# Sums of squares of a gated group norm: a row of ones as weights and a way through DRAM, in a one-core Mamba-2 kernel

## The chip, the cores and the metric

The kernel runs on one core of a Trainium2 chip, in fp32. The metric is the device time of one execution in microseconds (us): before the change 1738.12 us, the median of three runs (1737.26 to 1739.64). Smaller is better.

The core has five engines with an instruction list each: PE (TensorE, the matmuls; PEld are its weight loads), DVE (VectorE), ACT (ScalarE), POOL (GpSimd) and SP (SyncE, which only issues transfers). Each works its own list strictly in order; they wait for each other by semaphores. A transfer is issued from an engine's list, and whoever reads its data waits for its landing.

## The reference, cut to what matters

```python
y = (Y_diag + Y_off).reshape(b, l + pad, NH, HD) + D_res     # a Mamba-2 layer, 4 batches x 256 tokens
y = y[:, :l].reshape(b, l, DIN)                              # DIN = 8192
y = y * jax.nn.silu(gate)
yg = y.reshape(b, l, G, GROUP_SIZE)                          # G = 8 groups of 1024
var = jnp.mean(yg * yg, axis=-1, keepdims=True)
y = (yg * jax.lax.rsqrt(var + EPS)).reshape(b, l, DIN) * norm_w
return y @ out_proj_w.T
```

In front of it stands a layer norm and beside it an FFN with ternary weights, whose silu is multiplied to the result; they are not touched. The change concerns `var`: for each of 1024 tokens and each of 8 groups the sum of 1024 squares.

## The kernel before, in words

The 8192 channels are 64 tiles of 128 channels (partitions) by 1024 tokens; eight tiles are a group. After a front part (layer norm, FFN, B and C, early decay rows), a loop over the 64 tiles runs three stages shifted against each other. The program's order in each engine's list is written out by hand, so the order of the code is the order of the lists.

In step i:
- tile i is projected (`product`, L170, matmul at L173) by Strassen-like products into px, pq and pz; its convolution and silu follow on VectorE and ACT (L181, L186). The last product of pq (L173, "pq<-xnT,s") accumulates onto the pq that the add at L898 has read before;
- tile i-1 gets its sequence mixing: `decay_scan` (L188, a scan on VectorE) over the decay rows m that `load_rows` (L612, transfer at L617) fetched one step earlier, an exponential (L630), products with the scores (`meet`, L632), transposes through the one PSUM bank of the pool `ps_t`, the v products on VectorE (L648, L657), and `y_products` (L671, matmul at L684). From step 10 on the scan of tile i's first m is made at the beginning of step i (L850), before tile i-1's `meet`, and that of its second m at the end (L953);
- tile i-2 is gated (`y_gate`, L687), stored to DRAM (L825), squared on ACT (`square`, L862). The first square of a group is the tile sqacc; later ones are added to it by an accumulating transfer from POOL (L938);
- the finished group is projected by the output weights (`out_first`, L743, matmul at L740): factor sums of the loaded group on VectorE (`left_sums`, L808 and L720 to L723), then four products in an even and three in an odd step; ACT moves them out (L794), scaled by rs, into sa, sb and sc, and POOL adds them to DRAM. sc has two buffers.

A group ends so: steps 9, 17, 25, ... square its last tile. In the following step (10, 18, 26, ...) `norm_sums` (L699) makes eight matmuls with sqacc as weights and a column of ones as the moving side, so that the sums stand on the tokens' partitions, [128 x 8]; ACT takes the square root (L705), VectorE the reciprocal rs (L922), and ACT's leaves of that step use it. The eighth group is summed in the same way after the loop.

In SP's list, `load_rows` for step i+1 stands at the end of step i. Its first load needs a free buffer of five and goes out in the middle of step i; its second waits until `y_products` of step i has read tile i-1's m. Behind it stand the weights w and off-diagonal decay rows mo of the next step, and the store of the gated tile.

Of the kernel before, what the change touches and what calls it, by code (L numbers as in the profile page):

```python
# [43 lines left out]
F32 = mybir.dt.float32  # L44
# [3 lines left out]
ALU = mybir.AluOpType  # L48
PSUM = bass.MemoryType.PSUM

P = 128
NB = 4
L = 256
NC = 2
T = NB * L
NT = T // P
# [5 lines left out]
G = 8  # L62
# [3 lines left out]
CT = DIN // P  # L66
PER_G = CT // G
HG = PER_G // 2
HH = HID // 2
# [5 lines left out]
LEAD = 10  # L75
EARLY = 10
HALF = T // 2
ROW = T + NB * P


@with_exitstack
def mixer_ffn(ctx: ExitStack, tc: tile.TileContext, x, in_w, conv_w, conv_b, dt_bias, a_log, d_col,
              norm_w, out_w, gate_t, up_t, down_t, gate_s, up_s, down_s, out):
    nc = tc.nc

    const = ctx.enter_context(tc.tile_pool(name="const", bufs=1))
    small = ctx.enter_context(tc.tile_pool(name="small", bufs=3))
    dram = ctx.enter_context(tc.tile_pool(name="dram", bufs=1, space=bass.MemoryType.DRAM))
    ps_proj = ctx.enter_context(tc.tile_pool(name="ps_proj", bufs=3, space=PSUM))
    ps_t = ctx.enter_context(tc.tile_pool(name="ps_t", bufs=1, space=PSUM))  # L90
    ps_o = ctx.enter_context(tc.tile_pool(name="ps_o", bufs=2, space=PSUM))
# [2 lines left out]

    eps = const.tile([P, 1], F32, name="eps")
    nc.gpsimd.memset(eps, EPS)
    one = const.tile([P, 1], F32, name="one")
    nc.gpsimd.memset(one, 1.0)
    ident = const.tile([P, P], F32, name="ident")
    make_identity(nc, ident)  # L100
# [17 lines left out]
    dt_tail = mc.tile([P, NB, NH], F32, name="dt_tail")  # L118
    gm = mc.tile([P, ROW], F32, name="gm")
    xc = mc.tile([P, 4, KT // 2, HALF], F32, name="xc")  # L120
    xpad = mc.tile([P, NB, PADW], F32, name="xpad")
    nc.gpsimd.memset(xpad[:, :, 0:TAPS - 1], 0.0)
    rows = dram.tile([NH, ROW], F32, name="rows")
    ffn = dram.tile([T, HID], F32, name="ffn")
    acc = dram.tile([T, HID], F32, name="acc")
    gated = dram.tile([CT, P, T], F32, name="gated")
    early = dram.tile([2 * EARLY, P, T], F32, name="early")
    scores = dram.tile([G, P, ROW], F32, name="scores")

    def load_w(*tiles):  # L130
        w = wp.tile([P, 2, KT, P], F32, name="w")
        for n, i in enumerate(tiles):
            nc.sync.dma_start(w[:, n], in_w[i])
        return w
# [23 lines left out]

    x11, x12, x21, x22 = [xnT[:, k:k + 2, h:h + HALF] for k in (0, 2) for h in (0, HALF)]
    t1, t2, t3, t4 = [xc[:, n] for n in range(4)]  # L160

    def halves(xpad):
        return [xpad[:, 2 * h:2 * h + 2, TAPS - 1:] for h in range(2)]

    xpad_h = halves(xpad)

    def by_batch(v):
        return v.rearrange("p (b l) -> p b l", l=L)
# [23 lines left out]
    def front(pre, one_of, fp, f2, hp, ep):  # L192
# [11 lines left out]
        bT, cT = [one_of.tile([P, NB, L], F32, name=n) for n in ("bT", "cT")]  # L204
        sc = one_of.tile([P, ROW], F32, name="sc")
        wdt = one_of.tile([P, KT, P], F32, name="wdt")
# [69 lines left out]
        def split_x():  # L276
            return [hp.tile([P, KT, HALF], F32R, name=n) for n in ("xh", "xl")]

# [5 lines left out]
        def project_exact(w, xh, xl):  # L284
            pp = ps_proj.tile([P, HALF], F32, name="pp", tag="proj")
            for k in range(KT):
                for part in (xh, xl):
                    nc.tensor.matmul(pp, w[:, k * P:(k + 1) * P], part[:, k, :],  # L288
                                     start=(k == 0 and part is xh),
                                     stop=(k == KT - 1 and part is xl))  # L290
            return pp
# [26 lines left out]
        def dt_project(h):  # L318
            pd = ps_proj.tile([P, HALF], F32, name="pd", tag="proj")
            for k in range(KT):  # L320
                nc.tensor.matmul(pd, wdt[:, k, :], xnT[:, k, h * HALF:(h + 1) * HALF],  # L321
                                 start=(k == 0), stop=(k == KT - 1))
            nc.vector.tensor_scalar(z[:, h * HALF:(h + 1) * HALF], pd, bias, None, ALU.add)
# [285 lines left out]
    osp = main.enter_context(tc.tile_pool(name="osp", bufs=1, reuse_waits="tile"))  # L609
# [86 lines left out]

        return k // 2 if g in (0, G - 1) else max(k // 2, k - 2)

    def norm_sums(sqacc, pool=ps_o, tag="o"):  # L699
        pv = pool.tile([P, NT], F32, name="pv", tag=tag)  # L700
        for t in range(NT):
            nc.tensor.matmul(pv[:, t:t + 1], sqacc[:, t * P:(t + 1) * P], one,  # L702
                             start=True, stop=True)
        sd = small.tile([P, NT], F32, name="sd2")
        nc.scalar.activation(sd, pv, AF.Sqrt, bias=eps, scale=1.0 / (DIN // G))  # L705
        return sd


    def load_gated(g, b, tiles=PER_G):
        ya = yap.tile([P, PER_G, L], F32, name="ya")  # L710
        nc.sync.dma_start(ya[:, 0:tiles], gated[g * PER_G:g * PER_G + tiles, :,
                                                b * L:(b + 1) * L].rearrange("j p l -> p j l"))
        return ya
# [29 lines left out]
    def out_first(left, right, leave):  # L743

        a11, a12, a22, s1, s2, s4, s3 = left
        b11, b21, b22, tw1, tw2, tw3, tw4 = right
        px, pq = out_bank(), out_bank()
        out_product(px, a11, b11, True)
        yield leave(px, 0, 0, 0)
        out_product(pq, s1, tw1, True)  # L750
        yield leave(pq, 1, 1, 1)
        out_product(px, s2, tw2, False)
        yield leave(px, 0, 1, 0)
        out_product(pq, s4, b22, False)
        yield leave(pq, 0, 1, 1)

        out_product(px, s3, tw3, False)
        yield leave(px, 1, 1, 0)
        out_product(pq, a12, b21, True)
        yield leave(pq, 0, 0, 1)  # L760
        out_product(px, a22, tw4, False)
        yield leave(px, 1, 0, 0)
# [17 lines left out]
    with tc.manual_schedule():  # L780
        nc.sync.dma_start(gm, scores[0])
        ms, offs = {0: load_rows(0)}, {0: load_off(0)}
        xTs, gTs, yps, wos, rights, toms = {}, {}, {}, {}, {}, {}
        sqacc = sq = rs = ya = outs = left = nxt = ob = sa = sb = sc = None
        for i in range(CT):
            r, g = i % PER_G, i // PER_G
            here, old, older = True, i >= 1, i >= 2
# [20 lines left out]
            def left_sums():  # L808
                nonlocal ya, left
                ya = nxt  # L810
                left, sums = left_factors(ya)
                for make in sums:
                    make()

            if on % 2 == 0:
                ob = on // 2
# [6 lines left out]
            if older:  # L823
                yg = y_gate(yps.pop(i - 2), gTs.pop(i - 2))
                nc.sync.dma_start(gated[i - 2], yg.rearrange("p b l -> p (b l)"))  # L825
                if r == 1 and i >= PER_G and here:
                    nxt = load_gated((i - PER_G) // PER_G, 0)

            if here:
                a11, a12, a22, s1, s2, s4, s3 = a  # L830
                px, pq, pz = [p.tile([P, HALF], F32, name=f"p{n}", tag=tag) for n, p, tag in
                              (("x", ps_proj, "proj"), ("q", ps_proj, "proj"),
                               ("z", ps_proj if i else ps_t, "proj" if i else "t"))]
# [28 lines left out]
            def square():  # L862
                nonlocal sq, sqacc
                yf = yg.rearrange("p b l -> p (b l)")
                first = (i - 2) % PER_G == 0
                sq = sqp.tile([P, T], F32, name="sqacc" if first else "sq")
                nc.scalar.activation(sq, yf, AF.Square)  # L867
                if first:
                    sqacc = sq

            if older and fill:
                square()
# [6 lines left out]
            if old and fill:  # L879
                yps[i - 1] = y_begin(i - 1, xTs[i - 1])  # L880
            if og >= 0 and on == 0:
                sd = norm_sums(sqacc)
            for k in range(PER_G):
                if wg >= 0 and wn == come(wg, k) + 1:
                    wo = wos[wg][:, k, :]
# [3 lines left out]

            if og >= 0 and (here and on % 2 == 0 or i == CT - 1):
                left_sums()
            if wg >= 0 and wn == (PER_G - 1 if wg else PER_G - 3):
                rights[wg], toms[wg] = right_factors(wos[wg])
                toms[wg].pop(0)()
            if here:
                nc.vector.tensor_add(xpad_h[1], xpad_h[1], by_batch(pq))  # L898
            if old:
                vs = values_0(i - 1, tp0)  # L900
# [17 lines left out]
            if here:  # L918
                nc.vector.tensor_add(gT[:, HALF:], gT[:, HALF:], pq)
                if og >= 0 and on == 0:  # L920
                    rs = small.tile([P, NT], F32, name="rs2", bufs=2)
# [11 lines left out]
                    nc.scalar.activation(gT[:, HALF:], gT[:, HALF:], AF.Silu)  # L933
            if old:
                y_products(yps[i - 1], vs, ms.pop(i - 1), offs.pop(i - 1), fill)
            if older and (i - 2) % PER_G:
                if i - 2 < CT - 1:
                    nc.gpsimd.dma_start(sqacc, sq, accum_op=ALU.add)  # L938
                else:
                    nc.vector.tensor_add(sqacc, sqacc, sq)  # L940
            if here:
                conv_taps(i, xTs[i], xpad, (1, 2) if fill else (0, 1, 2))
                gTs[i] = gT
# [12 lines left out]
            if og >= 0 and on % 2:  # L956
# [3 lines left out]
                else:  # L960
                    nc.gpsimd.dma_start(rows_b, sa, accum_op=ALU.add)
                nc.gpsimd.dma_start(rows_b[:, 0, :], sb.rearrange("p n c -> p (n c)"),
                                    accum_op=ALU.add)
                nc.gpsimd.dma_start(rows_b[:, 1, HH:], sc, accum_op=ALU.add)
            elif og >= 0 and on < PER_G - 2:
                nxt = load_gated(og, ob + 1)
# [11 lines left out]
        last, ob = CT - 1, NB - 1  # L978
# [8 lines left out]
        sa = wp.tile([P, NC, KT, P], F32, name="w").rearrange("p n k m -> p n (k m)")  # L987
        sb = scp.tile([P, 3, KT // 2, P], F32, name="s")[:, 0:2].rearrange("p n k m -> p n (k m)")
        sc = osp.tile([P, HH], F32, name="sc", bufs=2)
        outs = out_first(left, rights[G - 2], leave)  # L990
# [3 lines left out]
        sq = sqp.tile([P, T], F32, name="sq")  # L994
# [10 lines left out]
        sq = sqp.tile([P, T], F32, name="sq")  # L1005
# [10 lines left out]
        left, sums = left_factors(yas[0])  # L1016
# [10 lines left out]

        whole[1] = fetch(1)
        yas[2] = load_gated(G - 1, 2)
        sd = norm_sums(sqacc, ps_t, "t")  # L1030
        rs = small.tile([P, NT], F32, name="rs2", bufs=2)
        nc.vector.reciprocal(rs, sd)
        for b in range(NB):
# [24 lines left out]
            left = ahead  # L1058
# [51 lines left out]
```

## Time and profile before

| what | value |
|---|---|
| median of 3 runs | 1738.12 us |
| the profiled execution's own time | 1738.69 us |
| its span, first to last instruction | 1737.0 us |
| matmuls of the sums of squares (L702), busy in all | 14.8 us, 128 records |
| L189, the scan of decay rows | 108 times, 2281 ns mean |
| loads of decay rows (m<-rows) | 108 times, 512 KB, 6.6 us median to landing |
| granted TensorE clock | 0.999 |

A page shows one profiled execution. Busy time of an engine, as a share of the span, tells how full its list is; the chain that ended last is followed back from the end, at each step to what released an instruction, and tells whose microseconds set the time. A line of the timeline gives start, length, engine, source line, operation, out<-in, shapes, and in brackets the idle time before it and what ended it. For "SPq" the length is from issue to the end of the issuing, waits of merged ones included. A matmul of fp32 is recorded as two instructions.

### The profile page before, as it was taken

The numbers are of one execution on the slowest core, as the hardware profiler recorded it, in microseconds if no ns is written. First come the engines' busy times: TensorE is split into PE (matmuls) and PEld (weight loads), VectorE is DVE, ScalarE is ACT, GpSimd is POOL, SyncE is SP. The second block draws the span as 40 slices with busy tenths as digits, with TensorE's granted clock in tenths as the row PEclk, the third lists the DMA queues.
The fourth block names the chain that finished last, engine by engine and source line by source line (L and its number), as shares of the span: only waits on it lengthen the run. The fifth ranks groups of instructions, "written<-read, shape, count | busy, mean of one in ns | idle before, by whom it ended". The sixth has DMA issues, their size and how long they took to land.

```text
span 1737.0 us, 22579 instructions
## 1 busy us (share of the span) xinstructions
PE 1720.0 (99%) x8494; PEld 1110.4 (64%) x8494; DVE 1447.2 (83%) x1742; ACT 1068.6 (62%) x1418; POOL 214.7 (12%) x238
## 2 busy tenths in 40 slices
PE   9999999999999999999999999999999999999999
PEld 7666667455566666666666666666666666666687
DVE  5768787687898898889888988898889888888876
ACT  4544333578766666666666666666666666667740
POOL 3222323000000000111011101110111011101110
PEclk9999999999999999999999999999999999999999
DMA  6246665667746675767677767766776677757785
GB/s 226 90 164 236 218 223 189 219 186 232 234 153 204 201 212 177 208 202 214 190 209 203 216 191 209 203 202 191 207 199 198 181 212 199 215 164 211 211 235 165
DMA packets 161931, 347.27 MB, mean 200 GB/s; under 512 B 15136, under 2 KB 52896, under 8 KB 161824
## 3 DMA queue, kind: packets, MB, share of 16 engines
q1 hardware_dynamic: 139136, 292.89, 48.6%
q0 software_dynamic: 22688, 52.96, 17.2%
q8 instruction: 67, 1.10, 0.2%
q14 instruction: 40, 0.33, 0.1%
HBM read 236.48 MB, written 81.00 MB: 183 GB/s over the span
## 4 chain that ended last, share of the span: by engine, by line
PE 90%; DVE 4%; ACT 3%; issue 1%; DMA 1%; SPq 0%; ACTq 0%
PE px L173 28%; PE po L740 22%; PE pq L173 13%; PE py L684 10%; PE pz L173 6%; PE pp L288 3%; PE tp L640 3%; PE pf L296 2%; DVE cT L181 1%; PE pg L466 1%; PE pv L702 1%; DVE em L189 1%; ACT xT L186 1%; ACT m L630 1%; PE pd L321 0%
## 5 line engine op out<-in xcount | busy, mean ns | idle before, releaser
L173 PE MATMUL px<-xc,w 128*128 128x512 f32 x576 | 272.7, 596 | 2.8 <-ACT gT L846 1.8
L181 DVE SCALAR_TENSOR_TENSOR xT<-xpad,cw,xT 128x1024 f32<-128x1024 f32 x192 | 246.0, 1281 | 13.8 <-ACT xT L177 9.6
L189 DVE TENSOR_TENSOR_SCAN m<-m,after 128x1024 f32<-128x1024 f32 x108 | 246.3, 2281 | 0.0
L740 PE MATMUL po<-wo,ya 128*128 128x256 f32 x768 | 176.5, 379 | 0.0
L633 DVE TENSOR_TENSOR m<-m,gm 128x1024 f32<-128x1024 f32 x128 | 154.8, 1210 | 21.1 <-ACT m L630 21.0
L684 PE MATMUL py<-m,v 128*64 128x128 f32 x2048 | 160.4, 276 | 0.0
L938 POOL DMA_DIRECT2D sqacc<-sq x54 | 46.1, 853 | 883.4 <-ACT sq L867 810.9
L740 PEld LDWEIGHTS po<-wo,ya 128*128 128x128 f32 x768 | 141.5, 190 | 17.0 <-issue 0.2
L173 PEld LDWEIGHTS px<-xc,w 128*128 128x128 f32 x576 | 99.3, 190 | 76.7 <-issue 68.9
L173 PE MATMUL pz<-xnT,w 128*128 128x512 f32 x288 | 145.8, 592 | 0.0
L173 PE MATMUL px<-xnT,w 128*128 128x512 f32 x288 | 141.8, 615 | 0.0
L173 PE MATMUL px<-xc,s 128*128 128x512 f32 x288 | 135.8, 594 | 2.4 <-ACT cpad L429 1.9
L173 PE MATMUL pq<-xc,s 128*128 128x512 f32 x288 | 135.5, 593 | 1.6 <-DVE sg L570 1.2
L173 PE MATMUL pq<-xnT,s 128*128 128x512 f32 x288 | 136.1, 595 | 0.1
L630 ACT ACTIVATE m<-m 128x1024 f32<-128x1024 f32 x128 | 135.4, 1058 | 0.7
L640 PEld LDWEIGHTS tp<-ident,xT 128*128 128x128 f32 x512 | 67.9, 141 | 100.0 <-issue 87.2
L684 PEld LDWEIGHTS py<-m,v 128*64 128x64 f32 x2048 | 117.1, 137 | 20.2 <-issue 19.1
L740 PE MATMUL po<-tw,sy 128*128 128x256 f32 x512 | 115.9, 379 | 0.0
L740 PEld LDWEIGHTS po<-tw,sy 128*128 128x128 f32 x512 | 97.2, 190 | 13.2
L846 ACT COPY gT<-px 128x512 f32<-128x512 f32 x64 | 37.3, 584 | 103.1 <-PE px L173 100.2
L173 PEld LDWEIGHTS pq<-xc,s 128*128 128x128 f32 x288 | 54.6, 190 | 71.2 <-issue 61.5
L684 PE MATMUL py<-mo,v 128*64 128x128 f32 x1024 | 99.4, 273 | 0.0
(177 smaller groups left out, 3125.6 us busy)
## 6 DMA issues: line engine op xcount, KB each, us to landing
m<-rows SPq DMA_DIRECT2D x108, 512.0 KB, 6.6
w<-in_in_w SPq DMA_DIRECT2D x144, 256.0 KB, 6.9
mo<-rows SPq DMA_DIRECT2D x128, 256.0 KB, 7.2
gated<-yg SPq DMA_DIRECT2D x64, 512.0 KB, 8.2
ya<-gated SPq DMA_DIRECT2D x30, 1024.0 KB, 7.1
sqacc<-sq POOLq DMA_DIRECT2D x54, 512.0 KB, 6.0
wo<-in_out_w SPq DMA_DIRECT2D x64, 256.0 KB, 7.0
acc<-sa POOLq DMA_DIRECT2D x23, 512.0 KB, 5.9
```

The lines of the kernel that those rows point to most:

```text
L173: nc.tensor.matmul(pp, a[:, k, :], b[:, k, :], start=start and k == 0, stop=k == KT // 2 - 1, skip_group_check=not start)
L181: nc.vector.scalar_tensor_tensor(xT, xpad[:, :, k:k + L], cw[:, i, k:k + 1], xT, ALU.mult, ALU.add)
L189: nc.vector.tensor_tensor_scan(m, m, after, 0.0, ALU.add, ALU.mult)
L288: nc.tensor.matmul(pp, w[:, k * P:(k + 1) * P], part[:, k, :], start=(k == 0 and part is xh), stop=(k == KT - 1 and part is xl))
L296: nc.tensor.matmul(pf, part[:, i * P:(i + 1) * P], wd, start=(f == 0 and part is hh), stop=(f == FT - 1 and part is hl))
L630: nc.scalar.activation(m, m, AF.Exp)
L633: nc.vector.tensor_mul(m, m, gm[:, 0:T])
L640: nc.tensor.transpose(tp[:, b, :], xT[:, b, c * P:(c + 1) * P], ident)
L684: nc.tensor.matmul(py[d, q * P:(q + 1) * P], v[:, b, h, :], m, start=False, stop=True, skip_group_check=True)
L740: nc.tensor.matmul(po, a[:, k, :], b[:, k, :], start=start and k == 0, stop=k == HG - 1, skip_group_check=not start)
L846: nc.scalar.copy(gT[:, HALF:], px)
L938: nc.gpsimd.dma_start(sqacc, sq, accum_op=ALU.add)
```

## The change

The sums of the first seven groups are made in another way, one step earlier; the eighth keeps the old one.
- The ones become a [128 x 32] tile and are the weights; sqacc is the moving side. Four products, one for each batch of 256 tokens, write 32 equal rows each into one [128 x 256] PSUM tile of `ps_t` (`norm_rows`). They stand directly behind `y_products` of the step that squares the group's last tile (9, 17, ..., 57).
- ACT copies the tile into a buffer of sc, SP stores four of its rows (one of each batch) to a DRAM tile, and SP loads them back as [128 x 8], one 4-byte element at a time. Both transfers are issued ahead of that step's `load_rows`.
- The square root in the next step (`norm_root`) reads the loaded tile; the eight matmuls in the middle of that step are gone.
- The accumulating transfer from POOL is written directly behind the square, not at the end of the step.
- In step 10 alone the add of pq to the padded tile stands ahead of the factor sums.

```diff
+SUMS = P // NB
-    one = const.tile([P, 1], F32, name="one")
+    one = const.tile([P, SUMS], F32, name="one")
+    sums_of = dram.tile([G, T], F32, name="sums_of")
...
+    def norm_rows(g, sqacc):
+        pr = ps_t.tile([P, L], F32, name="pr", tag="t")
+        for b in range(NB):
+            nc.tensor.matmul(pr[b * SUMS:(b + 1) * SUMS, :], one, sqacc[:, b * L:(b + 1) * L],
                              start=True, stop=True)
+        row = osp.tile([P, HH], F32, name="sc", bufs=2)
+        nc.scalar.copy(row, pr)
+        nc.sync.dma_start(sums_of[g].rearrange("(b i) -> b i", i=L), row[0:P:SUMS, :])
+        pv = small.tile([P, NT], F32, name="pvs")
+        nc.sync.dma_start(pv, sums_of[g].rearrange("(t p) -> p t", p=P))
+        return pv
+
+    def norm_root(pv):
         sd = small.tile([P, NT], F32, name="sd2")
         nc.scalar.activation(sd, pv, AF.Sqrt, bias=eps, scale=1.0 / (DIN // G))
         return sd
...
                 if first:
                     sqacc = sq
+                else:
+                    nc.gpsimd.dma_start(sqacc, sq, accum_op=ALU.add)
...
             if og >= 0 and on == 0:
-                sd = norm_sums(sqacc)
+                sd = norm_root(pvs)
...
+            if here and i == PER_G + 2:
+                nc.vector.tensor_add(xpad_h[1], xpad_h[1], by_batch(pq))
             if og >= 0 and (here and on % 2 == 0 or i == CT - 1):
                 left_sums()
...
-            if here:
+            if here and i != PER_G + 2:
                 nc.vector.tensor_add(xpad_h[1], xpad_h[1], by_batch(pq))
...
                 y_products(yps[i - 1], vs, ms.pop(i - 1), offs.pop(i - 1), fill)
-            if older and (i - 2) % PER_G:
-                if i - 2 < CT - 1:
-                    nc.gpsimd.dma_start(sqacc, sq, accum_op=ALU.add)
-                else:
-                    nc.vector.tensor_add(sqacc, sqacc, sq)
+            if older and (i - 2) % PER_G == PER_G - 1:
+                pvs = norm_rows((i - 2) // PER_G, sqacc)
             if here:
                 conv_taps(i, xTs[i], xpad, (1, 2) if fill else (0, 1, 2))
...
                 if i + 1 < CT:
                     ms[i + 1] = load_rows(i + 1)
```

## The prediction

> **What bounds the kernel now.** I read the page's engine line first, then the chain of work that ended last, then one group boundary engine by engine. A forecast is made against the profiled execution: span 1737.0 us, its own time 1738.69, which is 0.57 above the median of the runs shown (1738.12).
>
> ```profile
> span 1737.0 us, 22579 instructions
> PE 1720.0 (99%) x8494; PEld 1110.4 (64%) x8494; DVE 1447.2 (83%) x1742; ACT 1068.6 (62%) x1418; POOL 214.7 (12%) x238
> PE 90%; DVE 4%; ACT 3%; issue 1%; DMA 1%; SPq 0%; ACTq 0%
> ```
>
> TensorE has no idle time worth the name, so microseconds taken out of its list count in full, and so does any stall put into it. The chain around the boundary of step 17 and step 18 (its columns: start, length, what) holds TensorE alone. Here is the piece that the change removes:
>
> ```profile
> 644.77 2.77 PE py L684 x48
> 647.54 1.92 PE px L173 x4
> ...
> 656.77 1.68 PE pv L702 x16
> 658.45 1.82 PE px L173 x4
> 660.27 1.72 PE pq L173 x4
> ```
>
> Call T the end of Y's products, 647.54. The sums of squares stand at T+9.2 and cost 1.68 us. In the timeline of that stretch VectorE goes straight from gating into the scan of step 18's first decay rows, and then has no idle time until 661:
>
> ```profile
> 649.20 2.28 DVE L189 TENSOR_TENSOR_SCAN m<-m,after 128x1024 f32<-128x1024 f32 x1
> ...
> 657.51 0.68 DVE L898 TENSOR_TENSOR xpad<-xpad,pq 128x512 f32<-128x512 f32 x1
> ...
> 658.71 0.68 DVE L648 TENSOR_TENSOR v<-tp,dt_tail 128x512 f32<-128x512 f32 x1
> ```
>
> The add at L898 reads pq, and the last pq product accumulates onto the same pq, so TensorE's pq at 660.11 (timeline) may not begin before that add is done, at 658.19. The slack is **1.92 us**, and nothing waits for it today. Lastly SP, whose queue carries the scan's rows:
>
> ```profile
> 635.20 0.37 SPq L711 DMA_DIRECT2D ya<-gated  x1
> 635.62 12.05 SPq L617 DMA_DIRECT2D m<-rows  x2
> 647.76 0.39 SPq L959 DMA_DIRECT2D acc<-sa  x1
> ```
>
> The two loads of L617 are merged: the first goes out at 635.62, 13.6 us before its scan; the second waits for the buffer that Y's products read and goes at T. Median landing 6.6 us: the first is there by about 642, long before its use.
>
> **What goes and what comes, on TensorE.** 7 of 8 groups lose their 16 matmul records (1.68 us each, L702). They gain four products of ones against 256 columns, two records each, so 8 records. A record of 256 columns over the full width takes 6.91/32 = 0.216 us (po, L740 x32), one after another 1.73 us: nothing saved. Y's products write half of the rows each, and 48 records of 128 columns take 2.77 us, 0.058 each, where transposes of the same width take 0.44/4 = 0.11: two run side by side. At that rate the new products cost 8 x 0.115 = **0.92 us**; four abreast would be 0.46. I take 0.92, the measured rate, and keep 0.46 and 1.73 as ends. Gain: 0.76 x 7 = 5.3 us, if nothing waits.
>
> [...]
>
> The products need the last square added to sqacc. That transfer goes from POOL directly after the square today too (636.58, after a square that ends at 636.2), since POOL waits for nothing else; writing it earlier in the program moves nothing. It lands 9.4 us later, at 646.0: 1.5 us before T. Free by that much; the slowest of all 54 took 9.7.
>
> **ACT.** The copy of pr (0.47, the row of 128x256 leaves, 0.20 after TensorE) stands in ACT's list behind the last leave (ends 645.28) and ahead of L186. It cannot begin before T+1.1. L186 and the exponential behind it (1.14 + 1.28 table load + 1.06) run 645.18 to 648.69 today; they would end near T+5.1, 652.6, so pz's copy (0.57) ends at 653.2 instead of 650.1. The px product at 651.01 overwrites what it reads; 0.92 later by the new products it is due at 651.9 and would stall by some 1.2 us. It matters only if nothing later is later.
>
> **SP is where it is decided.** In the program's order of SP's queue the store of the row and the load of the sums stand *ahead of* both L617 loads of the next step. SP executes in order. The store waits for ACT's copy, the load waits until the store has landed. So the first L617 load, today issued at T-11.9, moves behind them. The links from T:
> - products 0.92 (0.46 to 1.73);
> - ACT 0.20 + 0.47 = 0.67;
> - store of 4 KB until landed: the smallest stores in the trace are 128 KB (out, median 1.7). I take 1.7, the upper end is 2.9 (early);
> - issue of the sums' load, 128x8 pieces as the ya loads have: 0.42. SP needn't wait for its landing;
> - landing of the first L617 load: the loads of L617 issued right at the seven boundaries took 4.8, 4.7, 6.6, 7.1, 6.6, 6.9, 6.9, mean 6.2, and I take that. Ends: 3.4, the fastest of 108, and 8.8: 7.1 plus 1.7, if the sums' load is in its way for as long as a small store takes.
>
> The scan can start at T + 0.92 + 0.67 + 1.7 + 0.42 + 6.2 + 0.1 = **T+10.0**; it starts at T+1.66 today. Queued behind it on VectorE are four products by gm, four factor sums and the add at L898. From the scan's start to the add's end is 8.99 us (649.20 to 658.19) without a gap, so the add ends at T+19.0, and pq starts at T+19.05 against T+12.57 (660.11): **+6.5 us**, with saved matmuls and ACT's stall already inside, because pq is now pinned to VectorE. It is not paid twice: from there TensorE needs 11.9 us to the end of Y's products, VectorE 12.8 to its last scan, of which 1.5 was waiting for pq, so VectorE is level again. Six such groups (steps 18 to 58): 39 us.
>
> The first group (step 10) has the add moved ahead of the factor sums, as the diff says. There T is 469.96, the landing row 4.8, so the scan starts at T+8.6 = 478.6, not 473.66. The add is no longer last; the second v product is (10.35 us after the scan's start, 473.66 to 484.01), and the transposes at 484.69 need it since they write the bank that it reads: 478.6 + 10.4 = 489.0, +4.3 us.
>
> The square root reads the sums at about T+11 (658.48 today); they land near T+6. Free. The borrowed sc buffer is overwritten in step 18 at 665.92, its last transfer goes out at 654.58 with a median landing of 9.5: free by 1.8 us, and more once step 18 is later.
>
> **Sum.** 39 + 4.3 = 43.3; 1738.69 + 43.3 = **1782 us**.
>
> **Rivals.**
> - *The cover holds, faster.* If the decay rows still reach VectorE by T+3.6 (1.66 plus the slack of 1.92), only TensorE's saving is left: 1738.7 - 5.3 = 1733.4. It needs copy, store, issue and load in 2.7 us; 1.7 and 3.4 are the fastest rows for two of them. Against it speaks also that SP stands still in its queue for 866 us in all, so nothing overtakes. 4 in 100.
> - *ACT is the limit, no change.* The rows are in time, but ACT's late copy of pz takes 1.2 x 6 back: 1738.7 - 5.3 + 7.2 = 1740.6. Same condition as before. 4 in 100.
> - *The delay runs on.* Step 19's rows, w and mo stand behind the same waits, and VectorE is level with TensorE by only some 0.7 us; if 2 us more are lost in the following step: 43 + 14 = 1796. 17 in 100.
> - *The products don't run side by side* (the change doesn't do what it says): the chain is 0.8 longer, +5.7: 1788. 10 in 100, and it lies inside the forecast's side.
> - The forecast: 65 in 100.
>
> **Numbers.** Low end, all links at their fast ends: scan at T+6.75, pq at T+15.8, +3.2 x 6, first group +2.4: 1760. High end, all slow: scan at T+14.6, +11.0 x 6, first group +10.2: 1815. The forecast's variants are all slower; this kernel can be told from no change by about 0.2% (3.5 us). Faster 0.04, same 0.04, slower 0.92.
>
> **What will show it.** At seven boundaries VectorE idle some 8 us before L189, ended by the load of m; TensorE idle 5 to 7 us before pq in six of them and before tp in the first; DVE and DMA in the chain of waits; the new products near 0.9 us; SP standing before the sums' load for about 2 us. It would be wrong if L617's loads went out before the store, if the store landed well under 1 us, or if VectorE's wait did not reach pq.

## The result, and the profile after

The changed kernel takes **1794.63 us** (median of 4, 1793.29 to 1795.26) against 1738.22 in the runs beside it: ratio 1.032 (95% interval 1.031 to 1.033), slower by 56 us. The forecast was 1782 in a range of 1760 to 1815: the direction and the place are right, and the size is 13 us short, for a reason that stood in none of its steps.

The page's first lines and the chain that ended last, of the kernel after. TensorE's share fell from 99% to 96%. In the chain DMA rose from 1% to 4%, two of its lines now by name, and VectorE from 4% to 7%:

```profile
span 1791.6 us, 22503 instructions
...
PE 1727.6 (96%) x8438; PEld 1102.8 (62%) x8438; DVE 1449.2 (81%) x1742; ACT 1069.3 (60%) x1425; POOL 217.0 (12%) x238
...
PE 84%; DVE 7%; DMA 4%; ACT 3%; issue 1%; SPq 0%; ACTq 0%; DVEq 0%
PE px L175 24%; PE po L759 22%; PE pq L175 12%; PE py L686 10%; PE pz L175 6%; PE pp L290 4%; PE tp L642 3%; DMA m<-rows 2%; PE pf L298 2%; DMA sums_of<-sc 1%; DVE m L635 1%; DVE cT L183 1%; DVE m L191 1%; PE pg L468 1%; DVE em L191 1%
```

The same boundary as in the forecast, now as the chain has it (start, length, what). It is no longer TensorE alone; read downwards it is the forecast's list of links, from the new products to the last pq:

```profile
651.47 0.61 PE pr L706 x8
...
652.11 0.38 ACT sc L709
...
652.50 1.61 DMA sums_of<-sc
...
654.17 0.37 SPq L712
...
654.60 4.99 DMA m<-rows
...
659.61 2.29 DVE m L191
...
668.02 0.61 DVE xpad L921
668.62 0.04 issue
668.67 3.78 PE pq L175 x4
672.45 0.85 PE tp L642 x4
673.30 7.74 PE po L759 x32
```

The waits (who waited for what, us in all, times, longest) show the same over the whole kernel. Those of VectorE:

```profile
DVE m L191 <- DMA m<-rows: 51.6, 7, 8.4
```

Those of TensorE, where pq's is the longest and ACT's late copy of pz the next:

```profile
PE pq L175 <- DVE xpad L921: 35.7, 6, 6.6
PE px L175 <- ACT pz L855: 4.6, 6, 0.8
...
PE tp L642 <- DVE v L650: 2.0, 1, 2.0
PE pr L706 <- DMA sqacc<-sq: 1.9, 1, 1.9
...
PE pq L175 <- DVE xpad L914: 1.8, 1, 1.8
```

And those of SP's list: the store waits for ACT's copy, the load for the store's landing:

```profile
SPq L710 <- ACT sc L709: 86.6, 7, 13.1
...
SPq L712 <- DMA sums_of<-sc: 15.7, 7, 3.0
```

Look once more at the end of that chain. The pq that begins late also takes longer: four records in 3.78 us, 1.72 before; the po behind it 7.74 against 6.91. No engine holds them up. A table by stretches (length, busy time of PE, PEld, DVE, ACT, POOL, then granted clock, DMA share and GB/s) tells why. First the kernel before, from pq to the end of Y's products; then two boundaries of the kernel after, each while waiting and after the wait:

```profile
660.00:672.00 12.00, 12.00 (x89) 9.64 (x87) 9.94 (x13) 8.17 (x11) 0.00 (x0) 1.00 0.02 4
```

```profile
652.00:668.60 16.60, 11.24 (x32) 4.71 (x28) 10.13 (x14) 10.60 (x14) 1.76 (x2) 0.98 0.82 243
668.60:682.00 13.40, 13.33 (x58) 9.81 (x60) 11.32 (x15) 5.89 (x9) 0.00 (x0) 0.77 0.03 5
836.90:854.90 18.00, 11.28 (x32) 4.74 (x28) 10.20 (x14) 10.60 (x14) 1.81 (x2) 0.93 0.82 224
854.90:869.00 14.10, 14.06 (x88) 10.67 (x88) 11.91 (x15) 7.57 (x10) 0.00 (x0) 0.85 0.01 1
```

The granted clock was 1.00 in that stretch before the change (0.999 over the whole run) and is 0.77 and 0.85 behind the two waits of the kernel after (0.987 over the whole run). In the clock's own records it is 0.5 for 6.8 us at five of the six later boundaries and for 10.2 us at the last, beginning during the wait. From pq's start to the next step it takes 13.6 to 15.1 us instead of 11.9, 15 us in the six together. The accounts: TensorE's added idle time 46.0 (35.7 + 1.8 + 2.0 + 1.9 + 4.6, the 1.8 being pq's wait in the first group), the slow clock 15.0, the saved matmuls -7 x (1.68 - 0.61) = -7.5. Sum 53.5, against 54.6 of longer span.

### The profile page after: what moved, and what is told of

It is laid out like the page before. It is cut to its first block, busy times and chain, and to the rows that moved or that the text cites. A ratio compares the mean times of both kernels' runs of the same rounds, so it can differ in the third digit from the quotient of the medians.

```text
span 1791.6 us, 22503 instructions
## 1 busy us (share of the span) xinstructions
PE 1727.6 (96%) x8438; PEld 1102.8 (62%) x8438; DVE 1449.2 (81%) x1742; ACT 1069.3 (60%) x1425; POOL 217.0 (12%) x238
## 4 chain that ended last, share of the span: by engine, by line
PE 84%; DVE 7%; DMA 4%; ACT 3%; issue 1%; SPq 0%; ACTq 0%; DVEq 0%
PE px L175 24%; PE po L759 22%; PE pq L175 12%; PE py L686 10%; PE pz L175 6%; PE pp L290 4%; PE tp L642 3%; DMA m<-rows 2%; PE pf L298 2%; DMA sums_of<-sc 1%; DVE m L635 1%; DVE cT L183 1%; DVE m L191 1%; PE pg L468 1%; DVE em L191 1%
## 5 line engine op out<-in xcount | busy, mean ns | idle before, releaser
L175 PE MATMUL pq<-xnT,s 128*128 128x512 f32 x288 | 147.4, 637 | 37.6 <-DVE xpad L921 35.7
L175 PEld LDWEIGHTS px<-xc,w 128*128 128x128 f32 x576 | 99.3, 190 | 76.7 <-issue 68.9
L175 PEld LDWEIGHTS pq<-xnT,s 128*128 128x128 f32 x288 | 54.8, 201 | 111.2 <-issue 54.5
L175 PEld LDWEIGHTS px<-xc,s 128*128 128x128 f32 x288 | 53.8, 190 | 76.3 <-issue 61.9
```

Of the source, the lines that this page charges most:

```text
L175: nc.tensor.matmul(pp, a[:, k, :], b[:, k, :], start=start and k == 0, stop=k == KT // 2 - 1, skip_group_check=not start)
```

## The experiments

Theory A: SP works its list in order, so the store and the load of the sums hold back the decay rows behind them, the late scan holds back the add, the add holds back pq, and after that idle stretch TensorE's clock is halved for a while. Theory B: the places of the new products and of ACT's copy cost the time. Theory C: the small transfers slow the others.

**Only SP's order undone.** Products and copy stay; the two transfers move behind the decay rows.

```diff
-        nc.sync.dma_start(sums_of[g]...)      # in norm_rows
-        pv = ...; nc.sync.dma_start(pv, sums_of[g]...)
...
                 if i + 1 < CT:
                     ms[i + 1] = load_rows(i + 1)
+                if older and (i - 2) % PER_G == PER_G - 1:
+                    pvs = norm_trip((i - 2) // PER_G, row)     # the same two transfers
```

> The changed kernel with one thing undone: the store of the row and the load of the sums stand behind both loads of decay rows in SP's list; products, copy, places and traffic stay. Theory A (SP's order holds the decay rows back, the late scan holds pq back, and TensorE then runs slow for a while): VectorE's wait for m before the scan (51.6 us in the changed kernel) falls to under 2, TensorE's wait for the add before pq (35.7) to under 2, granted clock back at 0.999. What stays is the 0.76 us before px in six steps and 1.9 in the first group, against 7 x 1.07 us of saved matmuls: about 1738.2 - 7.5 + 4.6 + 1.9 = 1737. Theory B (the place of the products and of ACT's copy costs the time): still about 1790. Theory C (the 4-byte pieces slow the other transfers): over 1780.

Measured 1738.03 (11 runs), ratio to before 1.0005 (0.9996 to 1.0014). All 56 us are gone. TensorE's longest waits in it:

```profile
PE px L175 <- ACT pz L858: 4.6, 6, 0.8
PE pr L706 <- DMA sqacc<-sq: 3.4, 1, 3.4
```

There is no wait of VectorE for m and no wait for the add any more. B and C fall: their causes are all still in this kernel. What it keeps (4.6, and a wait for the last square in the first group) is about as large as what it saves, so that the row of ones in this place is worth nothing. The profiled execution took 1742.06, 4 us above the median; its wait of 3.4 us for the last square is not there in every execution, as told below.

**Which of the two loads counts.** The first decay rows ahead of store and load, the second behind.

```diff
+                    ms[i + 1] = load_rows(i + 1, (0,))
+                    pvs = norm_trip((i - 2) // PER_G, row)
+                    ms[i + 1] += load_rows(i + 1, (1,))
```

> The changed kernel with the first load of decay rows ahead of store and sums' load, the second behind them. Theory A in its narrow form (only the first load counts, since the second one's scan stands at the end of the step): as with both loads ahead, about 1737, the second loads going out some 4 us later than T. If any wait ahead of the decay rows counts: between 1760 and 1794.

Measured 1738.40, ratio 1.0006 (0.9997 to 1.0016). SP of this kernel at the boundary:

```profile
635.12 0.57 SPq L619 DMA_DIRECT2D m<-rows  x1
648.28 0.53 SPq L713 DMA_DIRECT2D sums_of<-sc  x1
649.90 0.37 SPq L715 DMA_DIRECT2D pvs<-sums_of  x1
650.38 0.52 SPq L619 DMA_DIRECT2D m<-rows  x1
```

SP waits for the copy and for the store's landing as in the changed kernel, the second rows go out 3 us late, and it costs nothing. One 512 KB load on the wrong side of a wait, at each of seven boundaries, is the whole loss.

**The same transfers from POOL's list.**

```diff
-        nc.sync.dma_start(sums_of[g]...); nc.sync.dma_start(pv, sums_of[g]...)
+        nc.gpsimd.dma_start(sums_of[g]...); nc.gpsimd.dma_start(pv, sums_of[g]...)
```

> The changed kernel with store and load issued from POOL's list, everything else in its place, so that the same bytes move at the same point of the program but SP waits for nothing. Theory A: SP's list was the matter, so no waits for m, clock 0.999, about 1737, a few us more if POOL's own additions (sb, sc) come late. Theory C (the traffic): 1780 or more. Theory B (the place of products and copy): about 1790.

Measured 1738.50, ratio 1.0002 (0.9992 to 1.0011). The same bytes at the same place of the program cost nothing on another engine's list, though the load waits longer there (POOL's wait for the store is 37.0 us in all, SP's was 15.7). C falls a second time.

**The way through DRAM twice.**

```diff
+        nc.sync.dma_start(sums_of[g]...)          # behind the load: store again,
+        nc.sync.dma_start(pv, sums_of[g]...)      # load again, then the decay rows
```

> The changed kernel with the way through DRAM gone twice, load, store again and load again, all ahead of the decay rows; the second time writes and reads the same sums. Theory A: each boundary's scan is later by one more landing of a load (2.3 us) and of a store (about 3), so 5.3 x 7 = 37 us: about 1832, a few more if TensorE's slow stretch grows by a window. Theory B: no change, 1795. Theory C: the small pieces double, at most a microsecond for each boundary, under 1805.

Measured 1824.30, ratio 1.050 (1.048 to 1.052): 30 us more than the changed kernel, not 37. SP there:

```profile
655.90 0.51 SPq L710 DMA_DIRECT2D sums_of<-sc  x1
657.52 0.37 SPq L713 DMA_DIRECT2D pvs<-sums_of  x1
659.67 0.50 SPq L715 DMA_DIRECT2D sums_of<-sc  x1
661.29 0.36 SPq L713 DMA_DIRECT2D pvs<-sums_of  x1
661.71 1.05 SPq L619 DMA_DIRECT2D m<-rows  x2
```

The second trip costs 3.8 us here (657.52 to 661.29), since its store lands in 1.6, where I had put 3; it costs 4.0 at the first boundary and 5.1 to 5.3 at the other five, 33.8 in all. VectorE's wait for m grew to 81.3 us, by 29.7. The medians of the time are 29.7 apart, the two profiled executions 32.4. So nearly all of the delay in SP's list arrives in the time; where the rest of the 33.8 went was not followed up.

**The idle stretch filled.** Ten matmuls on constant data, whose results nobody reads, in TensorE's wait of steps 18 to 58.

```diff
+                if og > 0 and on == 0:
+                    idle = out_bank()
+                    for _ in range(10):
+                        nc.tensor.matmul(idle, xnT[:, 0, 0:P], xnT[:, 0, 0:HH], start=True, stop=True)
                 product(pq, s4, x22, False)
```

> The changed kernel with ten matmuls of 128x256 on constant data, whose results nobody reads, ahead of the last pq product in the six steps 18 to 58, about 4.3 us each, so that they lie in TensorE's wait of 4.7 to 6.7 us. Theory A, its second part (after the idle stretch TensorE is granted half its clock for 6.8 us, which costs 1.7 to 3.2 us from pq to the next step, 15 us in all): granted clock 0.997 or more, from pq to the next step 12.0 us as before the change, 1794.6 - 15 = 1780. If the slow stretch is not from the idleness: 1794.6 or a little more, clock still 0.987.

Measured 1779.76, ratio 1.024 (1.023 to 1.026): **15 us faster by adding work to the fullest engine**. TensorE of this kernel, and the two stretches in the columns used above:

```profile
665.40 4.48 PE L934 MATMUL po<-xnT 128*128 128x256 f32 x20
670.47 1.98 PE L176 MATMUL pq<-xnT,s 128*128 128x512 f32 x4 [0.58 <-DVE xpad L922]
```

```profile
654.00:670.40 16.40, 15.12 (x48) 8.24 (x46) 9.69 (x13) 10.27 (x14) 1.76 (x2) 1.00 0.86 247
670.40:682.50 12.10, 12.04 (x89) 9.76 (x89) 11.67 (x16) 7.62 (x10) 0.00 (x0) 1.00 0.02 3
```

VectorE is as late as before (its wait for m is 49.9 us), pq still waits for the add, and yet the clock is 1.00 in both stretches, 0.999 over the whole run, and pq to the next step takes 12.0 us. So the 15 us are the clock's, and the other 42 the wait itself.

**The add first in all seven steps**, not in step 10 alone.

```diff
-            if here and i == PER_G + 2:
+            if here and og >= 0 and on == 0:
```

> The changed kernel with the diff's own reordering (the add ahead of the factor sums) in all seven steps, not in the first alone. If pq is pinned to the end of the add: pq begins 2.65 us earlier in six steps, but the transposes behind it then wait for the second v product, which ends as late as before (some 1.25 us after the old add's end): transposes at T+19.8 instead of T+21 to T+22, so 1 to 2.4 us for each of six, 1780 to 1788; the wait moves from pq to tp. If the order on VectorE doesn't matter: 1794.6.

Measured 1782.86, ratio 1.025 (1.024 to 1.027): 12 us less than the changed kernel. TensorE's waits:

```profile
PE pq L175 <- DVE xpad L914: 21.5, 7, 4.1
PE tp L642 <- DVE v L650: 8.3, 7, 2.0
```

The wait before pq falls from 37.5 us in the seven to 21.5, and part of it comes back before tp, as it should if VectorE's list pins both. Of the 11.3 us between the two profiled spans, 1.9 are the wait for the last square, which this execution doesn't have. The diff's own reordering for step 10 is this remedy on one of seven boundaries; it shortens the loss and doesn't touch its cause.

**A version that keeps the gain.** The products move behind the first px of the next step, the copy behind pz's copy, and the transfers stand behind both decay rows and ahead of w.

```diff
-            if older and (i - 2) % PER_G == PER_G - 1:
-                pvs = norm_rows((i - 2) // PER_G, sqacc)     # behind y_products
...
+            if og >= 0 and on == 0:                          # next step, ahead of load_w
+                ... = head()                                 # px <- a11, x11; ACT: pz <- px
+                pvs = norm_trip(og, norm_rows(og, sqacc))
```

> The products stand one product later, behind the first px of the next step, ACT's copy behind pz's copy there, store and load behind the decay rows and ahead of w in SP's list. Theory A: no waits for m, no 0.76 before px, no wait for the last square in the first group; what is left is 7 x 1.07 us of saved matmuls: 1738.2 - 7.5 = 1731. The rival: the sums land too late for the square root (it is due at T+9.3, store and load need some 5 us from T+3), ACT waits and gives the gain back: 1735 to 1745.

Measured **1732.80**, ratio to before 0.9970 (0.9959 to 0.9982): faster than both kernels by 0.3% and more. Its page has TensorE at 1709.7 us of busy time in a span of 1730.2, 99%. The boundary on TensorE and ACT; nothing waits for the new work:

```profile
646.74 1.98 PE L175 MATMUL px<-xnT,w 128*128 128x512 f32 x4
648.65 0.64 PE L706 MATMUL pr<-sqacc,one 128*32 128x256 f32 x8
649.22 1.98 PE L175 MATMUL pq<-xc,s 128*128 128x512 f32 x4
651.04 1.88 PE L175 MATMUL px<-xc,s 128*128 128x512 f32 x4
```

```profile
648.76 0.57 ACT L847 COPY pz<-px 128x512 f32<-128x512 f32 x1 [0.80 <-PE px L175]
649.36 0.37 ACT L709 COPY sc<-pr 128x256 f32<-128x256 f32 x1
```

The square root begins at 657.65 without a wait, so the rival, sums that land too late, does not hold. The gain is 5.2 us by the medians, of 7.5 that the saved matmuls are worth and that I had expected in full; the span is 6.8 shorter than that of before. In the trace steps 18 to 58 are 1.02 us shorter each, nearly all that the matmuls save, but step 10 only by 0.17, since there tp waits 1.1 us for the second v product. The rest of the difference is within the 3.4 us that the runs of this kernel spread over.

## Why the prediction was right, and where it was short

- *SP decides*: right, and shown by three kernels that change nothing but the order or the engine of two transfers. The loads of L617 do stand behind the wait, and only the first of them matters.
- *The links*: scan at T+10.0 forecast, T+8.1 to T+10.1 measured, 9.4 in the mean. The sum came out near by luck, for two links were wrong and cancelled each other: the store of 4 KB landed in 1.6 us at the first of the six boundaries and in 3.1 to 3.6 at the other five (1.7 forecast), the decay rows in 4.8 to 5.1 (6.2 forecast). The difference between those boundaries is that in the first of them the output sums are not yet being added by POOL's transfers; that this slows the store is argued from their being in flight, and was not tried by itself.
- *The products*: 0.92 us forecast, 0.61 measured, between the forecast's value for two abreast and its estimate of 0.46 for four, which no run shows. At the six later boundaries the timeline has no idle time of TensorE directly before or behind them (651.40 and 651.97 at the first), so their shape, weights of 128x32 between 128x64 and 128x128, costs no wait that the trace shows.
- *Pinned to the end of the add*: right. pq starts 0.05 us after it, and comes 4.6 to 6.6 us later after T than before, 35.5 us in the six together, where 6.5 each and 39 were forecast. ACT's stall was forecast at 1.2 and measured at 0.8; it is absorbed in the changed kernel, as said, and once SP's order was mended it took 4.6 of the 7.5 us saved.
- *"From there TensorE needs 11.9 us to the end of Y's products"*: **this is the step that failed.** It needs 13.6 to 15.1, for its clock is at half for 6.8 us and, at the last boundary, 10.2, of which 3.2 to 6.2 us lie after the wait. That is 15 us, more than the whole error of 13. I had priced the stall as idle time alone, and taken the speed of the matmuls behind it from a trace without such a stall.
- *First group*: +4.3 forecast, +4.9 measured (steps 9 and 10 together). Its parts differ: 1.9 us are a wait of the products for the last square, which I had held free; its transfer took 9.2 us instead of the 5.8 of the trace before, which left some 1.7 us to spare. The wait differs from one execution to the next: of the seven kernels with the products in this place, the traces show 1.8, 1.9 and 3.4 us in three, 0.1 in one and none in three. Why the transfer is late in some is not known. The forecast had named 9.7 as the slowest of all 54, so this was a margin to be priced, not to be ticked off.
- *The rival "the delay runs on"* gave 1796, almost the measured time, for a reason that is wrong: the steps that follow take 21.05 and 22.81 us as before; nothing is late there.

## What to carry to other kernels

A small transfer whose issue waits is dear by what stands behind it in the list of the engine that issues it, here by 56 us with the first decay rows behind it and by none with only the second: put it behind every load that is needed sooner, or on a list where nothing urgent follows. Ask of each stall of a full TensorE not only how long it is but whether it also costs the clock; then it is paid with a surcharge, here a third (15.0 us on 46.0). And before a saving is put in place, look for the place where its inputs are already there and its readers not yet waiting: here it was one product later, and worth 0.3%.

## What the runs showed of the hardware

- In the changed kernel the granted clock is 0.5 in pieces of 3.41 us, two of them at five of the six later boundaries and three at the last; from 310 us to the end of the main loop it is 1.00 elsewhere. TensorE's waits before pq at the six are 4.66, 6.00, 5.99, 6.65, 6.00 and 6.45 us in order, so a wait's length alone does not decide: the one of 6.65 has two pieces, the one of 6.45 three. Waits of 1.9, 1.8 and 2.0 us in the first group (before pr, pq and tp) left the clock at 1.00. Where a wait lies may count too: in this trace the pieces begin whole multiples of 3.413 us apart (at 668.03, 852.35 and 1036.67 us, 54 pieces from one to the next). Lay this grid over its main loop. The six pieces at full clock that a slow one followed had TensorE idle for a share of 0.65 to 1.00; all others at full clock had 0.56 or less. The seven slow pieces that another slow one followed had a share of 0.19 to 1.00, the six that full clock followed 0.05 or less.
- Across the profiled executions the mean granted clock is lower where TensorE's waits for the add before pq, summed over the seven boundaries, are longer: 0.999 with none (the kernel before) and with 8.3 us (longest 1.8, idle stretch filled), 0.991 with 21.5 (longest 4.1, the add first), 0.987 with 37.5 (longest 6.6, the changed kernel), 0.976 with 68.9 (longest 11.6, the way through DRAM twice).
- Four fp32 products of 32 columns, 8 records of 256 columns, take 0.61 us; at the full width, one after another, they would take an estimated 1.73, 8 x 6.91/32 by the row of po in the kernel before.
- A load of 1024 single elements of 4 bytes landed in 2.2 to 2.3 us from SP in the changed kernel, little more than the 1.7 of a 128 KB store. Behind both loads of decay rows in SP's list it took 3.3 at the median, from POOL 3.5.
